# A two-layer graph kernel: waits between stores and between TensorE and VectorE dropped, scatters and loads moved on their queues, and the quantile products placed 22 sorting steps later

## The chip, the cores and the metric

The kernel runs on one core of a Trainium2 chip. A core has five engines with a queue each: TensorE (PE, with its weight loads shown apart as PEld), VectorE (DVE), ScalarE (ACT), GpSimd (POOL) and SyncE (SP), and DMA queues that SP, ACT and POOL start. The metric is the device time of one execution in microseconds (us); what is quoted is the median of several runs. The profile is of one execution of its own.

## The reference, cut to what matters

There are N = 4096 nodes with D = 128 features and a symmetric 0/1 adjacency matrix in which about 1.6% of the entries are set (some 64 neighbours for a node). The first layer is graph attention with 8 heads:

```
Wh  = einsum('nd,hde->hne', nodes, W)
f1, f2 = Wh·a1, Wh·a2
e   = leaky_relu(f1[:, :, None] + f2[:, None, :], 0.2)
att = softmax(where(adj > 0, e, -9e15), axis=-1)
h   = elu(att @ Wh)                       # 8 heads, concatenated: cat
x1  = layernorm(nodes + elu(cat @ W1 + b1))
```

The second layer takes, for each node and feature, three quantiles over the kept neighbours (every m-th neighbour of a list is left out; n_keep remain):

```
svals = sort(where(keep[:, :, None], x1[None, :, :], big), axis=1)
agg   = sum over q in (0.25, 0.5, 0.75) of svals[max(ceil(q * n_keep) - 1, 0)] / 3
agg   = 0.5 * agg + 0.5 * x1
out   = agg @ W.T + b + x1
```

All is in float32 or with integer indices.

## The kernel before, in words

**Stage one, `gat`** (up to about 3,160 us). The nodes are cut into 32 tiles of 128 and into six blocks of 4, 4, 6, 6, 6 and 6 tiles. Two jobs run interleaved.

One is the search for the neighbour lists (class `Front`). SP loads the adjacency in 128 pieces (`a_i`, L378), ScalarE turns them into 0/1 (`nz`, L380), TensorE packs bits into words (L389), and VectorE draws the column numbers out of the words with its instructions for the eight largest (L188, L190). When a block's lists are complete, `place` scatters them to a table `rows_d` in memory (POOL, L541), and further on `keep` makes the lists for the second layer, `meta_d`. This work is cut into some 90 pieces, which `advance(n)` takes from a list `todo`, n at a time; each piece writes its instructions at that place in the program. When all is found, `order` sorts the nodes by the length of their lists, and `late`, 32 calls of `scatter` (L680), writes the sorted order to `order_d`, one POOL DMA for each tile.

The other is attention. It goes over 64 half tiles u. `load(u + 3)` gathers the rows of neighbours three half tiles ahead (POOL, `nb`, L971: 2190 indirect DMAs in all, about 34 for a half tile); at the first tile of a block it also loads the block's list of ids from `rows_d` over SP (L903, and `info`, L932), and `own_row` gathers the nodes' own rows (`me`, L947). `probabilities` makes the softmax (VectorE L1054 to L1103, ScalarE L1073), `rows_sum` multiplies with the rows on TensorE (`ps_z`, L1111), and after two tiles `combine`, a generator of several stages, makes the head outputs, the layer norm, and as its last stage stores the new rows to `x1_d` by two indirect DMAs of POOL (L1197; "x_d" in the profile). After each half tile stands `advance(2)`. `late` is issued when the loads have run out, from u = 61 on, but without an order of its own: the scheduler places it on POOL's queue where its data is ready, and so it stands among the gathers of about 1,920 to 2,027 us.

At the end of `gat` the stages still open are driven to their end. Then a flag is read and a branch taken: to `general` if the lists don't fit the tables (not with this data), else to `sparse`.

**Stage two, `sparse`.** The order is loaded from `order_d` by four DMAs of SP. For each of the 32 tiles in that order, `load(t)` gathers the tile's table row (`info`, POOL L1867), its own rows (`xs`), and HIGH[t] rows of neighbours (`rows`, POOL L1713: 2078 of them), into one of three rotating buffers. A sorting network then runs over the rows' buffer: a step compares k blocks of 128 columns with k others. `compare` copies the lower side into a bank of PSUM on ScalarE (L1751; `low`, two buffers of 16 x 128 columns, or `low_s` in SBUF where k is at most 4), and VectorE writes the minimum (L1756) and the maximum (L1757) back. Steps of which only one side is needed take one instruction and no copy (L1759, L1761). `plan(t)` cuts the network into a first and a second phase, with steps of at most 16 pairs (8 for tile 0); `interleave` orders the second phase of tile t-1 with the first of tile t by modelled times.

After a tile's second phase `quantile` finds the candidates for the three quantiles and weights that are 1 or 0. `pick` returns three parts: `scale` (ScalarE multiplies the candidates by their weights, L1810), `sums` (TensorE adds them up and adds half of x1, L1815 and L1818), and a copy to `comT` (L1823). After four tiles `finish` adds `layer` (three products for each tile, L1835 to L1837) and `layer_copy` (copy to `o`, L1841, and four scatters to `out` on POOL, L1845). These parts wait in a first-in-first-out list, `waiting`. Each two-sided step takes at most one part from its head, right after ScalarE's copy: a part marked "copy" always, a part marked "bank" only where 4 < k <= 12, since it needs the last four of the bank's sixteen column blocks. What is left at the end is issued after the last step.

Of the kernel before, what the change touches and what calls it, by code (L numbers as in the profile page):

```python
# [38 lines left out]
F32 = mybir.dt.float32  # L39
F16 = mybir.dt.float16  # L40
BF = mybir.dt.bfloat16
I32 = mybir.dt.int32
# [3 lines left out]
ALU = mybir.AluOpType  # L46
# [4 lines left out]
P = 128  # L51
N = 4096
# [37 lines left out]
SMALL = 4  # L90
FOUR = 4
CUT = 32
MOST = 16

ENDS = [(t - t % FOUR, FOUR) for t in range(NT - FOUR)]
ENDS += [(NT - FOUR, FOUR - 1)] * (FOUR - 1) + [(NT - 1, 1)]
# [697 lines left out]
    return out  # L794


def gat(tc, nc, c, x, adj, xf_d, meta_d, order_d, flag_d, w, a1, a2, w1, b1, gamma, beta, x1_d):

# [22 lines left out]
    with ExitStack() as ctx:  # L823
# [307 lines left out]
        def combine(t, zT):  # L1131
# [62 lines left out]
            nc.vector.tensor_add(s, s, bc["beta"].unsqueeze(1).to_broadcast(shape))  # L1194
            yield
            for j in range(TWO):
                nc.gpsimd.indirect_dma_start(  # L1197
                    out=x1_d,
                    out_offset=bass.IndirectOffsetOnAxis(ap=index[t + j][3][:, 0:1], axis=0),
                    in_=s[:, j, :],  # L1200
                    in_offset=None,
                )

        held = {u: load(u) for u in range(3)}
        advance(EARLY)
        f1s = {0: spread_f1(0)}
# [3 lines left out]
        for u in range(2 * NT):  # L1210
            t, half = divmod(u, 2)
            if u + 3 < 2 * NT:
                held[u + 3] = load(u + 3)
            elif late:

                advance(len(todo))
                for piece in late:
                    piece()
                late = []
            if not half and t + 1 < NT:  # L1220
                f1s[t + 1] = spread_f1(t + 1)
            ps_z, behind = rows_sum(u, held.pop(u), e)
            if u + 1 < 2 * NT:
                with ExitStack() as order:
                    for ins in behind:
                        order.enter_context(tc.issue_after(ins))
                    e, behind = probabilities(u + 1, held[u + 1], f1s[(u + 1) // 2])
            with ExitStack() as order:
                for ins in behind:
                    order.enter_context(tc.issue_after(ins))  # L1230
                if u % (2 * TWO) == 0:
                    zT = tp.tile([P, H, TWO * P], F32, name="zT")
                collect(u, ps_z, zT)
                for stages in going:
                    next(stages, None)
            if u % (2 * TWO) == 2 * TWO - 1:
                going = going[-1:] + [combine(t - 1, zT)]
            advance(2)
        for stages in going:
            for _ in stages:  # L1240
                pass
        advance(len(todo))


def statistics(tc, nc, c, f_sb, f2m, rows_d):
# [412 lines left out]
def plan(t):  # L1658

    wide = HIGH[t]  # L1660
    extra = wide - MAIN if MAIN < wide <= 80 else 0
    w = wide - extra
    needed = {i - 1 for lo, hi in places(t) for i in range(lo - extra, hi + 1)}
    layers = needed_swaps(swap_layers(w), needed)
    merge = (w - 1).bit_length()

    first = steps(layers[:-merge], lambda i: i, PAIRS if t else PAIRS // 2)
    second = steps(layers[-merge:], lambda i: i)
    if extra:
        apart = needed_swaps(swap_layers(extra), range(extra))  # L1670
        first += steps(apart, lambda i: MAIN + extra - 1 - i)
    return first, second, extra


def sparse(tc, nc, c, x1_d, meta_d, order_d, w, b, out):


    with tc.tile_pool(name="sp1", bufs=1) as one, tc.tile_pool(
# [12 lines left out]
        sixth = one.tile([P, P], F32, name="sixth_i")  # L1691
        nc.scalar.mul(sixth, c["idf"], 0.5 * float(np.float32(1.0 / NQ)))
        wT = one.tile([P, D], F32, name="lwT")
        it = one.tile([P, 2 * MIDDLE], I32, name="it_p")
        nc.gpsimd.iota(it, pattern=[[1, 2 * MIDDLE]], base=0, channel_multiplier=0)
        iota_p = one.tile([P, 2 * MIDDLE], F32, name="iota_p")
        nc.vector.tensor_copy(iota_p, it)
        order = one.tile([P, NT], I32, name="order")
        for i in range(4):
            nc.sync.dma_start(  # L1700
                out=order[:, ts(i, NT // 4)],
                in_=order_d[ts(i, N // 4), :].rearrange("(t p) c -> p (t c)", p=P),
            )

        def bank():
            return psum.tile([P, PAIRS * D], F32, name="low")

# [2 lines left out]
        nc.scalar.copy(wT, ps[:, :D])  # L1710

        def gather(row, info, col):
            nc.gpsimd.indirect_dma_start(  # L1713
                out=row,
                out_offset=None,
                in_=x1_d,
                in_offset=bass.IndirectOffsetOnAxis(ap=info[:, col : col + 1], axis=0),
            )
# [19 lines left out]
        def compare(rows, step):  # L1738


            shape, d, low, high, _ = step
            lows, highs = block(rows, shape), block(rows, shape, d)
            if low and high:
                _, n2, _, n, _, run = shape
                k = n2 * n * run
                if k > SMALL:
                    t = bank()
                else:
                    t = tp.tile([P, SMALL * D], F32, name="low_s", bufs=4)
                packed = block(t, (0, n2, n * run, n, run, run))  # L1750
                nc.scalar.copy(packed, lows)  # L1751
                if waiting and waiting[0][0] == "copy":
                    waiting.pop(0)[1]()
                elif waiting and SMALL < k <= PAIRS - FOUR:
                    waiting.pop(0)[1](t[:, (PAIRS - FOUR) * D :])
                nc.vector.tensor_tensor(lows, packed, highs, op=ALU.min)  # L1756
                nc.vector.tensor_tensor(highs, packed, highs, op=ALU.max)  # L1757
            elif low:
                nc.vector.tensor_tensor(lows, lows, highs, op=ALU.min)  # L1759
            else:  # L1760
                nc.vector.tensor_tensor(highs, lows, highs, op=ALU.max)  # L1761
# [41 lines left out]
        def pick(found, x1, comT):  # L1803

            made = {}

            def scale():
                made["v"] = tp.tile([P, MOST, D], F32, name="picked", bufs=1)
                for i, (v, weight) in enumerate(found):
                    nc.scalar.mul(made["v"][:, i, :], v, weight)  # L1810

            def sums(ps):
                made["ps"] = ps[:, :P]
                for i in range(len(found)):
                    nc.tensor.matmul(  # L1815
                        made["ps"], made["v"][:, i, :], sixth, start=i == 0, stop=False
                    )
                nc.tensor.matmul(made["ps"], x1, half, start=False, stop=True)  # L1818

            return [  # L1820
                ("copy", scale),
                ("bank", sums),
                ("copy", lambda: nc.scalar.copy(comT, made["ps"])),  # L1823
            ]

        def finish(xs, comT, infos):

            m = len(infos)
            made = {}

            def layer(ps):
                made["ps"] = ps
                for j in range(m):
                    to = ps[:, ts(j, D)]
                    nc.tensor.matmul(to, c["idf"], xs[:, j, :], start=True, stop=False)  # L1835
                    nc.tensor.matmul(to, c["ones"][0:1, :], b_row[:, j, :], start=False, stop=False)
                    nc.tensor.matmul(to, comT[:, j, :], wT, start=False, stop=True)  # L1837

            def layer_copy():
                o = tp.tile([P, FOUR, D], F32, name="o")  # L1840
                nc.scalar.copy(  # L1841
                    o[:, :m, :].rearrange("p t d -> p (t d)"), made["ps"][:, : m * D]
                )
                for j, info in enumerate(infos):
                    nc.gpsimd.indirect_dma_start(  # L1845
                        out=out,
                        out_offset=bass.IndirectOffsetOnAxis(ap=info[:, NODE : NODE + 1], axis=0),
                        in_=o[:, j, :],
                        in_offset=None,
                    )  # L1850

            return [("bank", layer), ("copy", layer_copy)]
# [3 lines left out]
        def load(t):  # L1856
            rows = three.tile([P, max(HIGH), D], F32, name="rows")
            first, _ = ENDS[t]
            if t == first:
# [2 lines left out]
                    tp.tile([P, FOUR, P], F32, name="comT"),  # L1862
                    [],
                )
            info = three.tile([P, MW], I32, name="info", bufs=3 * FOUR)
            group[first][2].append(info)
            nc.gpsimd.indirect_dma_start(  # L1867
                out=info,
                out_offset=None,
                in_=meta_d,  # L1870
                in_offset=bass.IndirectOffsetOnAxis(ap=order[:, t : t + 1], axis=0),
            )
            gather(group[first][0][:, t - first, :], info, NODE)
            for s in range(HIGH[t]):
                gather(rows[:, s, :], info, s)
# [377 lines left out]
def gnn(tc, x, adj, w, a1, a2, w1, b1, gamma, beta, lw, lb, out):  # L2253
    nc = tc.nc
    with ExitStack() as ctx:
# [6 lines left out]

        keep = ctx.enter_context(tc.tile_pool(name="keep", bufs=1))
        c = constants(nc, keep)
        gat(tc, nc, c, x, adj, xf_d, meta_d, order_d, flag_d, w, a1, a2, w1, b1, gamma, beta, x1_d)
        other = nc.values_load(flag_d[0:1, 0:1], min_val=0, max_val=1)
        with tc.If(other > 0) as cmp:
            general(tc, nc, c, x, adj, w, a1, a2, w1, b1, gamma, beta, lw, lb, x1_d, out)
        with cmp.Else():
            sparse(tc, nc, c, x1_d, meta_d, order_d, lw, lb, out)  # L2270


_INS = [
# [33 lines left out]
```

## Time and profile before

| | before |
|---|---|
| median of 3 runs | 8432.01 us (8431.48 to 8434.64) |
| the profiled execution | 7646.96 us, of which the span is 7645.2 us |
| instructions | 31290 |
| busy: VectorE | 5831.7 us (76%) |
| busy: GpSimd | 4343.5 us (57%) |
| busy: ScalarE | 2214.1 us (29%) |
| busy: TensorE | 1122.8 us (15%) |
| granted TensorE clock, mean | 0.551 |

The profiled execution is 785 us shorter than the median of the runs. In the lines of the profile, L12 is line 12 of the kernel. A busy row has one digit for each fortieth of the span, 191 us: the busy share in tenths. A line of a group gives the engine, what it writes and reads, how often, then the busy time and the mean in ns of one, then the idle time ahead of the group's instructions, and what ended most of it. A line of the waits gives who waited for whom, the total in us, how many waits, and the longest. A line of the timeline gives start and length in us, and in brackets the idle time before with its releaser; "issue" means that the engine waited for nothing that the profile shows. A DMA that POOL starts shows as POOL's time for issuing it; its landing is later.

### The profile page before, as it was taken

The numbers are of one execution on the slowest core, as the hardware profiler recorded it, in microseconds if no ns is written. First come the engines' busy times: TensorE is split into PE (matmuls) and PEld (weight loads), VectorE is DVE, ScalarE is ACT, GpSimd is POOL, SyncE is SP. The second block draws the span as 40 slices with busy tenths as digits, with TensorE's granted clock in tenths as the row PEclk, the third lists the DMA queues.
The fourth block names the chain that finished last, engine by engine and source line by source line (L and its number), as shares of the span: only waits on it lengthen the run. The fifth ranks groups of instructions, "written<-read, shape, count | busy, mean of one in ns | idle before, by whom it ended". The sixth has DMA issues, their size and how long they took to land. (4 is left out here: it accounts for less than half of the span.)

```text
span 7645.2 us, 31290 instructions
## 1 busy us (share of the span) xinstructions
PE 1122.8 (15%) x6047; PEld 946.8 (12%) x6047; DVE 5831.7 (76%) x9380; ACT 2214.1 (29%) x2301; POOL 4343.5 (57%) x4524
## 2 busy tenths in 40 slices
PE   3243333322222322100000000000000000000001
PEld 1232222222222222100000000000000000000000
DVE  8465555565223222399999999999999999999999
ACT  6020212100000000144344343434334433443433
POOL 2777677777777777565554645455536434554500
PEclk5566666666566666655555555555555555555555
DMA  6242324222222222111111111111101101111100
GB/s 205 57 121 56 107 62 121 60 55 56 47 56 56 56 56 56 40 44 34 40 35 30 41 31 37 30 36 34 38 23 41 34 24 33 36 35 29 33 1 1
DMA packets 219057, 380.95 MB, mean 50 GB/s; under 512 B 129283, under 2 KB 129412, under 8 KB 218852
## 3 DMA queue, kind: packets, MB, share of 16 engines
q0 software_dynamic: 145808, 308.58, 15.3%
q1 hardware_dynamic: 72898, 70.23, 3.1%
q14 instruction: 156, 1.28, 0.1%
q8 instruction: 49, 0.80, 0.0%
q10 hardware_dynamic: 146, 0.07, 0.0%
HBM read 368.26 MB, written 10.31 MB: 50 GB/s over the span
## 5 line engine op out<-in xcount | busy, mean ns | idle before, releaser
L1713 POOL DMA_INDIRECT rows<-x_d,info x2078 | 2018.2, 971 | 1949.5 <-ACT picked L1810 1270.8
L971 POOL DMA_INDIRECT nb<-xf_d,ids x2190 | 2086.0, 953 | 707.0 <-issue 632.2
L1751 ACT COPY low<-rows 128x2048 f32<-128x2048 f32 (+8 forms) x1022 | 1561.5, 1533 | 2429.9 <-DVE rows L1757 1780.7
L1756 DVE TENSOR_TENSOR rows<-low,rows 128x2048 f32<-128x2048 f32 (+9 forms) x1022 | 1884.7, 1862 | 138.9 <-ACT low L1751 50.0
L1757 DVE TENSOR_TENSOR rows<-low,rows 128x2048 f32<-128x2048 f32 (+9 forms) x1022 | 1882.4, 1861 | 5.8
L1054 DVE TENSOR_TENSOR e<-nb,ps_small 128x64 f32<-128x64 f32 (+9 forms) x200 | 47.7, 240 | 1252.6 <-DMA nb<-xf_d,ids 1206.7
L1111 PE MATMUL ps_z<-spread,nb 128*128 128x128 f32 x4500 | 615.7, 305 | 797.9 <-DVE spread L1103 775.6
L1111 PEld LDWEIGHTS ps_z<-spread,nb 128*128 128x128 f32 x4500 | 604.5, 220 | 829.9 <-DVE spread L1103 420.7
L1815 PE MATMUL low<-sixth_i,picked 128*128 128x128 f32 x300 | 79.8, 442 | 4224.7 <-ACT low L1751 3736.4
L1815 PEld LDWEIGHTS low<-sixth_i,picked 128*128 128x128 f32 x300 | 66.8, 324 | 4237.7 <-ACT low L1751 3744.8
L1073 ACT ACTIVATE ps_e<-e 128x256 f32<-128x256 f32 (+4 forms) x64 | 26.1, 408 | 1936.2 <-DVE e L1054 972.6
L1103 DVE TENSOR_TENSOR spread<-e,ps_small 128x1152 f32<-128x1152 f32 (+4 forms) x312 | 342.7, 1107 | 129.2 <-PE ps_z L1111 79.4
L1845 POOL DMA_INDIRECT out<-o,info x32 | 34.4, 1076 | 392.9 <-ACT o L1841 369.2
L380 ACT ACTIVATE nz<-a_i 128x1024 bf16<-128x1024 int32 x128 | 134.3, 1051 | 292.5 <-DMA a_i<-in_adj 254.3
L1751 ACT COPY low_s<-rows 128x512 f32<-128x512 f32 (+3 forms) x325 | 139.8, 471 | 130.5 <-DVE rows L1756 48.0
L389 PE MATMUL ps_words<-nz,pows 128*128 128x512 bf16 (+1 forms) x272 | 113.7, 577 | 364.4 <-ACT nz L387 258.0
L188 DVE MAX8 k<-key 128x8 f32<-128x256 f32 x416 | 164.6, 412 | 0.7
L1756 DVE TENSOR_TENSOR rows<-low_s,rows 128x512 f32<-128x512 f32 (+3 forms) x325 | 158.3, 500 | 3.0 <-ACT low_s L1751 2.1
L1757 DVE TENSOR_TENSOR rows<-low_s,rows 128x512 f32<-128x512 f32 (+3 forms) x325 | 158.7, 500 | 0.3
L190 DVE MATCH_REPLACE8 key<-k,key 128x256 f32<-128x256 f32 x384 | 155.5, 407 | 0.0
L1142 PE MATMUL ps_h<-zT,w_ga 128*128 128x256 f32 x256 | 116.3, 619 | 198.4 <-DVE s L1414 106.6
L1759 DVE TENSOR_TENSOR rows<-rows 128x256 f32<-128x256 f32 (+8 forms) x245 | 141.6, 580 | 0.2
(246 smaller groups left out, 2528.0 us busy)
## 6 DMA issues: line engine op xcount, KB each, us to landing
a_i<-in_adj SPq DMA_DIRECT2D x128, 512.0 KB
nb<-xf_d,ids POOLq DMA_INDIRECT x2190, 2.5
rows<-x_d,info POOLq DMA_INDIRECT x2078, 2.5
xf_d<-xf POOLq DMA_DIRECT2D x4, 576.0 KB, 7.4
xf<-in_x POOLq DMA_DIRECT2D x4, 512.0 KB
meta_d<-rowdata_k SPq DMA_DIRECT2D x4, 324.0 KB
abc_ta<-in_L_gnn_a POOLq DMA_DIRECT2D x2, 512.0 KB, 7.7
w_ga<-in_L_gnn_W POOLq DMA_DIRECT2D x2, 512.0 KB
```

The lines of the kernel that those rows point to most:

```text
L188: nc.vector.max(out=top, in_=work)
L190: nc.vector.match_replace(out=work, in_to_replace=top, in_values=work, imm_value=gone)
L380: nc.scalar.activation(nz[:, j, :], a_i, AF.Relu, scale=-1.0, accum_out=self.negative[:, k : k + 1],)
L971: gather = nc.gpsimd.indirect_dma_start(out=rows[:, used + i, :], out_offset=None, in_=xf_d, in_offset=bass.IndirectOffsetOnAxis(ap=ids[:, ...
L1103: last = nc.vector.tensor_tensor(spread[:, :m], e[:, at : at + m, :].unsqueeze(2).to_broadcast(shape), own.unsqueeze(1).unsqueeze(3).to_br ...
L1111: product = nc.tensor.matmul(ps_z[:, g, :], rows[:, k, :D], spread[:, i].rearrange("p j h -> p (j h)"), start=i0 + i == 0, stop=i0 + i == ...
L1713: nc.gpsimd.indirect_dma_start(out=row, out_offset=None, in_=x1_d, in_offset=bass.IndirectOffsetOnAxis(ap=info[:, col : col + 1], axis=0),)
L1751: nc.scalar.copy(packed, lows)
L1756: nc.vector.tensor_tensor(lows, packed, highs, op=ALU.min)
L1757: nc.vector.tensor_tensor(highs, packed, highs, op=ALU.max)
L1759: nc.vector.tensor_tensor(lows, lows, highs, op=ALU.min)
L1815: nc.tensor.matmul(made["ps"], made["v"][:, i, :], sixth, start=i == 0, stop=False)
```

## The change

1. The stores of x1 are declared independent of each other (`stored`, `declare_no_dep`).
2. The 32 scatters of `order_d` are forced behind the last gather of `nb` in the issue order.
3. `advance(2)` becomes `advance(3)` for u < 16.
4. The constants `it_p` and `iota_p`, the `order` and the `info` of tiles 0 and 1 go to a pool that lives from the start. The loads of the order and the two gathers of `info` stand ahead of the last stages of the last `combine`, thus ahead of the branch; in `sparse`, `load` issues no `info` for these two tiles.
5. In `compare`, the minimum and the maximum of a step are declared independent of the products that TensorE makes in other columns of its bank. `sums` and `layer` return their products for that.
6. Between `scale` and `sums`, 22 parts that do nothing are put into `waiting` (APART); each two-sided step takes one.
7. `plan(0)` cuts the first phase of tile 0 into steps of at most 4 pairs instead of 8.
8. MOST, the room for scaled candidates, is 14 instead of 16; at most 14 are found.

```
-MOST = 16
+MOST = 14
+
+APART = 22
...
-                nc.gpsimd.indirect_dma_start(
+                done = nc.gpsimd.indirect_dma_start(
                     out=x1_d,
...
+                for other in stored:
+                    tc.declare_no_dep(done.ins, other, reason="each node has a row of its own")
+                stored.append(done.ins)
...
                 advance(len(todo))
-                for piece in late:
-                    piece()
+                with tc.issue_after(gathers[2 * NT - 1][HALF - 1, 0]):
+                    for piece in late:
+                        piece()
...
-            advance(2)
-        for stages in going:
+            advance(3 if u < 2 * START[2] else 2)
+        for stages in going[:-1]:
             for _ in stages:
                 pass
-        advance(len(todo))
+
+        for i in range(4):
+            nc.sync.dma_start(
+                out=order[:, ts(i, NT // 4)],
+                in_=order_d[ts(i, N // 4), :].rearrange("(t p) c -> p (t c)", p=P),
+            )
+        for t, info in enumerate(infos):
+            nc.gpsimd.indirect_dma_start(
+                out=info,
+                out_offset=None,
+                in_=meta_d,
+                in_offset=bass.IndirectOffsetOnAxis(ap=order[:, t : t + 1], axis=0),
+            )
+        for stages in going[-1:]:
+            for _ in stages:
+                pass
...
-    first = steps(layers[:-merge], lambda i: i, PAIRS if t else PAIRS // 2)
+    first = steps(layers[:-merge], lambda i: i, PAIRS if t else PAIRS // 4)
...
                 nc.scalar.copy(packed, lows)
+                aside = []
                 if waiting and waiting[0][0] == "copy":
                     waiting.pop(0)[1]()
                 elif waiting and SMALL < k <= PAIRS - FOUR:
-                    waiting.pop(0)[1](t[:, (PAIRS - FOUR) * D :])
-                nc.vector.tensor_tensor(lows, packed, highs, op=ALU.min)
-                nc.vector.tensor_tensor(highs, packed, highs, op=ALU.max)
+                    aside = waiting.pop(0)[1](t[:, (PAIRS - FOUR) * D :])
+                for to, op in ((lows, ALU.min), (highs, ALU.max)):
+                    done = nc.vector.tensor_tensor(to, packed, highs, op=op)
+                    for product in aside:
+                        tc.declare_no_dep(done.ins, product, reason="other columns of the bank")
...
             return [
                 ("copy", scale),
+                *[("copy", lambda: None)] * APART,
                 ("bank", sums),
                 ("copy", lambda: nc.scalar.copy(comT, made["ps"])),
             ]
```

## The prediction

> **What bounds the kernel now.** I read the busy slices first, then the costliest groups, the table of stretches, the waits, and the timeline of single places.
>
> ```profile
> DVE  8465555565223222399999999999999999999999
> POOL 2777677777777777565554645455536434554500
> ...
> L1713 POOL DMA_INDIRECT rows<-x_d,info x2078 | 2018.2, 971 | 1949.5 <-ACT picked L1810 1270.8
> L971 POOL DMA_INDIRECT nb<-xf_d,ids x2190 | 2086.0, 953 | 707.0 <-issue 632.2
> ```
>
> There are two stages. Up to slice 17 (about 3,200 us) VectorE (DVE) is half busy; GpSimd (POOL) is 70 to 80% busy in issuing the gathers of neighbours (L971), and nearly all the rest of its time is its own issue gap. From slice 18 on VectorE is over 90% busy with sorting and POOL's gathers (L1713) wait for free buffers. The stretches give the rate of the first stage:
>
> ```profile
> 400.00:600.00 200.00, 89.43 (x500) 73.08 (x500) 138.19 (x580) 55.07 (x86) 148.07 (x157) 0.66 0.43 119
> ...
> 800.00:1000.00 200.00, 72.75 (x387) 57.51 (x388) 131.91 (x576) 51.95 (x82) 125.85 (x130) 0.62 0.34 98
> ...
> 2200.00:2400.00 200.00, 61.51 (x379) 56.66 (x380) 61.46 (x147) 13.66 (x26) 151.23 (x161) 0.62 0.22 56
> ```
>
> After the stretch stand PE, its loads, DVE, ACT, POOL. A full stretch holds 160 gathers of 0.94 us with 0.30 us between: 1.25 us each, and nothing else fits. Every other POOL instruction among them lengthens the stage by itself; 800 to 1,000 us lost 30 gathers to stalls.
>
> ```profile
> POOL nb L971 <- PE ps_z L1111: 36.9, 8, 21.6
> POOL x_d L1197 <- DMA x_d<-s,info: 14.7, 8, 3.2
> POOL me L947 <- DMA info<-rows_d: 12.3, 3, 4.2
> DVE rows L1756 <- PE low L1837: 20.3, 8, 3.3
> DVE rows L1756 <- PE low L1818: 12.3, 10, 2.2
> SPq L903 <- DMA rows_d<-rowdata,pos_i: 299.0, 5, 95.0
> ```
>
> Total us, number, longest. The first three are POOL's real stalls in stage one, the next two VectorE's waits on TensorE in sorting, the last SP's wait for a block's lists. Then the join of the stages, on POOL:
>
> ```profile
> 3105.62 0.94 POOL L971 DMA_INDIRECT nb<-xf_d,ids  x1 [0.30 <-issue]
> 3146.65 0.98 POOL L1197 DMA_INDIRECT x_d<-s,info  x1 [40.09 <-DVE s L1194]
> 3149.16 0.97 POOL L1197 DMA_INDIRECT x_d<-s,info  x1 [1.52 <-DMA x_d<-s,info]
> 3154.85 0.96 POOL L1197 DMA_INDIRECT x_d<-s,info  x1 [4.72 <-DVE s L1194]
> 3158.36 0.96 POOL L1197 DMA_INDIRECT x_d<-s,info  x1 [2.55 <-DMA x_d<-s,info]
> 3162.02 0.23 POOL L1695 IOTA it_p<- 128x128 int32 x1 [2.71 <-issue]
> ...
> 3170.57 0.94 POOL L1713 DMA_INDIRECT rows<-x_d,info  x1 [0.30 <-issue]
> ```
>
> The last neighbour row leaves at 3105.62; POOL idles 40.09 us for the last rows' result, stores four times, passes the branch, builds indices, and gathers its first row to sort 64.95 us after it.
>
> [...] at 3149.16 POOL stands 1.52 us behind a store with nothing passing it. [...] The kernel has such waits between its stores, though each writes rows of its own; they are the 14.7 us above. [...]
>
> **Part by part**, against the profiled execution's own 7646.96 us (span 7645.2). That is 785 us below the runs' median 8432.01; nothing in the profile says why.
>
> *Order scatters.* Now 32 scatters of order_d stand among the gathers:
>
> ```profile
> L680 POOL DMA_INDIRECT order_d<-node,pos_g x32 | 30.8, 962 | 9.8 <-issue 8.8 <-DMA order_d<-node,pos_g 0.6 <-DVE e L1063 0.3
> ```
>
> (30.8 + 9.8) = 40.6 us of a full POOL. Moved behind the last gather they fill the 40.09 us of idleness: −40.6. Without that cover they would cost all of it again.
>
> *Stores of x1.* The waits between stores go: 14.7 listed and two of 1.5 that the waits book to VectorE, less 1.52 and 2.55 at the join, which are counted below: −13.6.
>
> *The join.* From the last gather: scatters start at 1.25, the last at 1.25 + 31 x 1.27 = 40.6; a scatter landed a median 3.6 us after issue (2.2 to 5.8): 44.2. SP's four loads of the order (0.4 to issue, 2.4 to land): 47. Two info gathers, 47.2 to 49.7. The four stores queue behind them on POOL; their second pair's data is ready at 49.2 in the trace, so they go at 1.25 us: last at 53.5, landed 3.2 later, branch 0.5 (as now), one gather of own rows: first row at 58.4 instead of 64.95: −6.5. What is late next is VectorE's last normalisation, if scatters are quicker.
>
> *A third piece per half tile for u < 16.* In stage one VectorE does 12.5 us of attention per half tile (50 us per 200 us, 43.3 us of POOL per half tile) and pieces of the neighbour lists, 72 in about 608 us: 8.4 each. With three: 12.5 + 25.3 = 37.8 of 43.3 us, 87%. It fits on average, and lists are written earlier: the scatter of block 2's lists stands behind gather 333 instead of 480, of block 1's behind 158 instead of 194. That meets the stalls' root: On SP, L903 waits for the scatter (it now stands behind 87 adjacency loads instead of 79), holds back the loads of the adjacency behind it, and ScalarE with them:
>
> ```profile
> 793.18 1.06 ACT L380 ACTIVATE nz<-a_i 128x1024 bf16<-128x1024 int32 x1 [71.77 <-DMA a_i<-in_adj]
> 799.18 0.46 DVE L1074 TENSOR_TENSOR ps_e<-e,ps_e 128x288 f32<-128x288 f32 x1 [39.36 <-ACT ps_e L1073]
> ```
>
> VectorE then loses 39 us and POOL stalls 8.49 and 21.61 at 820 and 883. Stalls on ps_z over 0.6 us sum to 35.7, on info 12.3: 48 in all. Bounds: −48 (all gone) to +134 (all 16 pulled-forward pieces, 8.4 each, delay POOL). I take −15: a third, since the fuller VectorE makes new ones.
>
> *Waits of sorting on TensorE.* The instruction order shows 39 steps waiting for TensorE before, none after: −(20.3 + 12.3) = −32.6. The wait can move to ScalarE: the copy of a result (comT, o) comes right behind the next step's copy, and the layer's 24 products take 7.9 us (4224.45 to 4232.3). ScalarE has slack (slices of 40%) and sums come 24 to 28 steps, about 80 to 110 us, after the scaling, so their data is never late; I put back 7.6 for eight layers: −25. Bounds −32.6 and 0. Empty pops cost nothing: they emit no instruction.
>
> *Tile 0 in steps of 4 pairs.* 83 steps with 99.1 us of VectorE for 46 with 88.6 (counted from the plan, with the trace's times): +10.5 of work, but VectorE idles 20.10, 10.07 and 13.95 us for rows there, and smaller steps start on fewer rows. −5, bounds −10 and +10.5.
>
> *Tail.* 22 steps behind, the last loop's 14 both-sided steps run out: the sums of tile 30, its copy, the last full layer and its output fall behind the last comparison at 7632.88. Nine products at 0.67 (6 us), and output scatters that go 2.8 us apart, partly beside the last tile's: +5, bounds +2 and +10.
>
> Preload and pool moves else cost nothing: the index constants (0.23 us on POOL) now start the kernel beside loads.
>
> Sum: −40.6 −13.6 −6.5 −15 −25 −5 +5 = −100.7, to 7546 in the profile's execution. On the runs, −101 if a stall is as long there, −111 if the 10% is spread evenly: 8432 − 106 = about 8326; I say 8325.
>
> **Rivals.**
> *A, everything goes:* stalls 48, waits 32.6, tile 0 −10, tail +2, the rest the same: −149, about 8280. For it: block 2's lists are 147 gathers (184 us) earlier. Against: VectorE at 87%.
> *B, the waits come back:* TensorE's wait becomes ScalarE's (0), stalls stay (0), tile 0 +10.5, tail +10, the rest −60.7: −40, about 8390. [...] Against: its slack.
> *C, VectorE becomes the bound early:* 87% busy leaves 5.5 us per half tile, 88 us over 16. If ScalarE's stalls (39 to 48 us each, three in the trace) remain, or pieces cost over 10.3 us each beside (12.5 + 3 x 10.3 = 43.3), POOL waits for spread matrices, and the pulled-forward pieces show in full: +134 − 101 = +33, about 8465. Against: the pieces gone from later halves leave nothing to overfill, and POOL runs three half tiles ahead.
> *D, the change doesn't do what it says:* scatters still among gathers, or the waits kept. The built order speaks against it; at most some effects cancel, 8432.
>
> **How the numbers follow.** Forecast (−60 to −135) 0.62, 8325; A (to −185) 0.13, 8280; B (−20 to −60) 0.13, 8390; C 0.07, 8465; D 0.05. About 0.2% (17 us) is what a measurement tells from no change. Range 8250 to 8412 holds the forecast, B and most of A; C, D and A's end are out, 0.15. Faster 0.88, same 0.05, slower 0.07.
>
> **What would show it.** Full stretches of 160 gathers around 1,950 us and 32 scatters behind the last gather; no POOL wait for a store; first sorting gather about 58 us after the last neighbour row; no VectorE wait on TensorE; last tile's products, one full layer and its outputs behind the last comparison. It is wrong if POOL's waits on ps_z grow in 200 to 900 us, if VectorE's waits on ScalarE grow by as much as those on TensorE fall, or if the tail passes 20 us.

## The result, and the profile after

The changed kernel took 8382.62 us (8371.12 to 8386.41), the kernel before 8433.33 (8431.48 to 8440.11): ratio 0.9939, interval 0.9924 to 0.9954. That is 51 us faster, where 107 were forecast. The profiled execution took 8386.41 us, span 8384.6. It agrees with the runs, which the profile before did not. One thing must be known to read any number below: executions come in two kinds, one in which the kernel before takes 8377 to 8433 us and one in which it takes 7644 to 7648, and the profile before is of the second kind, the result of the first. The page of the changed kernel, first kind:

```profile
DVE  6454564454222222224899999999999999999899
...
POOL 3545546656666666666455456445554545354410
...
L1726 POOL DMA_INDIRECT rows<-x_d,info x2078 | 2031.9, 978 | 1863.7 <-ACT picked L1826 1184.2
L975 POOL DMA_INDIRECT nb<-xf_d,ids x2190 | 2078.1, 949 | 1329.5 <-issue 625.3
```

Stage one now reaches slice 18 of longer slices: the last neighbour gather leaves at 3739 us instead of 3106. A gather costs POOL what it did (949 ns, 953 before), and its own issue gap is the same (625 us, 632 before); to that come 704 us of other idleness, where there were 75. The stretches and the waits say where they are:

```profile
400.00:600.00 200.00, 53.68 (x316) 43.38 (x315) 114.47 (x499) 46.72 (x74) 95.53 (x101) 0.62 0.30 87
800.00:1000.00 200.00, 48.89 (x206) 37.33 (x206) 97.77 (x424) 34.47 (x53) 112.59 (x119) 0.59 0.26 74
2200.00:2400.00 200.00, 66.21 (x306) 58.09 (x307) 49.33 (x124) 11.17 (x21) 129.56 (x138) 0.59 0.19 48
```

```profile
POOL nb L975 <- PE ps_z L1115: 508.2, 33, 58.5
POOL nb L975 <- remote: 170.6, 36, 9.4
```

No stretch is full any more (101, 119, 138 instructions of POOL where 160 fit): POOL waits 679 us for buffers that TensorE has yet to read. ("Remote" is a release whose origin the profile doesn't show; 35 of these 36 waits are on a semaphore that in this trace TensorE alone raises.) TensorE's own lines at one place of stage one, where the profile shows nothing that it waits for:

```profile
2185.80 1.95 PE L1115 MATMUL ps_z<-spread,nb 128*128 128x128 f32 x16
2188.36 0.27 PE L1115 MATMUL ps_z<-spread,nb 128*128 128x128 f32 x1 [0.61 <-issue]
2191.16 0.27 PE L1115 MATMUL ps_z<-spread,nb 128*128 128x128 f32 x1 [2.53 <-issue]
2193.96 0.37 PE L1115 MATMUL ps_z<-spread,nb 128*128 128x128 f32 x1 [2.53 <-issue]
2196.75 0.37 PE L1115 MATMUL ps_z<-spread,nb 128*128 128x128 f32 x1 [2.42 <-issue]
...
2210.05 0.37 PE L1115 MATMUL ps_z<-spread,nb 128*128 128x128 f32 x1 [0.33 <-issue]
2210.75 0.37 PE L1115 MATMUL ps_z<-spread,nb 128*128 128x128 f32 x1 [0.33 <-issue]
2211.45 1.87 PE L1115 MATMUL ps_z<-spread,nb 128*128 128x128 f32 x8 [0.33 <-issue]
```

After 16 products in 1.95 us one comes every 2.80 us, with a weight load halfway (the first at 2189.75): an instruction every 1.40 us. Later the products come 0.70 us apart, then eight in 1.87 us. I call such a stretch the grid. ScalarE and VectorE fall on it too: at tile 0, shown below, their starts after a wait are 1.40, 4.20 or 5.60 us apart. The profile before has no such gap at any of its products; summed over the trace, the gaps of this kind (0.3 to 2.6 us, at products that wait for nothing) are 592 us here.

### The profile page after: what moved, and what is told of

The parts are those of the page before. It is cut to its first block, busy times and chain, and to the rows that moved or that the text cites. A ratio compares the mean times of both kernels' runs of the same rounds, so it can differ in the third digit from the quotient of the medians.

```text
span 8384.6 us, 31455 instructions
## 1 busy us (share of the span) xinstructions
PE 1235.7 (15%) x6047; PEld 1032.2 (12%) x6047; DVE 5886.7 (70%) x9454; ACT 2218.9 (26%) x2338; POOL 4358.1 (52%) x4524
## 5 line engine op out<-in xcount | busy, mean ns | idle before, releaser
L1771 DVE TENSOR_TENSOR rows<-low,rows 128x2048 f32<-128x2048 f32 (+10 forms) x1970 | 3649.3, 1893 | 88.0 <-ACT low L1764 61.7
L1764 ACT COPY low<-rows 128x2048 f32<-128x2048 f32 (+8 forms) x985 | 1528.4, 1557 | 2331.8 <-DVE rows L1771 1665.3
L1115 PE MATMUL ps_z<-spread,nb 128*128 128x128 f32 x4500 | 757.9, 325 | 1491.4 <-issue 737.3
L1115 PEld LDWEIGHTS ps_z<-spread,nb 128*128 128x128 f32 x4500 | 702.4, 237 | 1565.9 <-issue 996.7
L1771 DVE TENSOR_TENSOR rows<-low_s,rows 128x512 f32<-128x512 f32 (+3 forms) x798 | 395.3, 523 | 128.7 <-remote 39.9
L1764 ACT COPY low_s<-rows 128x512 f32<-128x512 f32 (+3 forms) x399 | 179.8, 486 | 281.6 <-DVE rows L1771 172.0
L1873 POOL DMA_INDIRECT out<-o,info x32 | 34.9, 1091 | 397.2 <-ACT o L1869 369.3
L1130 ACT COPY zT<-ps_z 128x512 f32<-128x512 f32 x64 | 37.6, 587 | 742.7 <-remote 586.0
L190 DVE MAX8 lists<-cand 128x8 f32<-128x176 f32 x416 | 128.1, 332 | 69.7 <-remote 47.1
L1438 DVE SCALAR_TENSOR_TENSOR zT<-zT,ps_h 128x512 f32<-128x512 f32 x64 | 42.0, 682 | 158.0 <-ACT zT L1437 109.7
```

Source lines behind the costliest of these rows:

```text
L190: nc.vector.max(out=top, in_=work)
L1115: product = nc.tensor.matmul(ps_z[:, g, :], rows[:, k, :D], spread[:, i].rearrange("p j h -> p (j h)"), start=i0 + i == 0, stop=i0 + i == ...
L1771: done = nc.vector.tensor_tensor(to, packed, highs, op=op)
```

## The experiments

The runs form five sets, each on a chip of its own beside the kernel before, and all runs of a set met the same kind. Sets one and two (chips 2 and 5) met the first kind, with the grid; three and four (chips 1 and 15) the second, without; five (chip 10) the first again.

**The kernel before, unchanged.**

> The kernel before, unchanged, for a profile in the state of the timed runs. Theory G (grid): the profile of the changed kernel shows stretches in which TensorE, and ScalarE and VectorE too, start one instruction every 1.40 us; the timed runs of the kernel before have them too and its profile of 7647 us lacks them. Then this profile is about 8430 us long, its last neighbour gather leaves at about 3750 to 3800 us instead of 3106, POOL waits some 600 us on ps_z in stage one, and stage two is about as long as in the changed kernel, 4500 to 4550 us. Rival S (stage two): the first stage gained what was forecast and the change itself lengthened sorting by some 80 us. Then the last gather leaves near 3850 us and stage two takes about 4450 us.

8388.47 us beside 8389.51; span 8372.6. The last neighbour gather left at 3643.8, POOL waited 561 us for TensorE (369.3 on ps_z, 191.5 "remote"), TensorE's slow gaps are 631 us. So the grid is there without the change, as theory G said, though the last gather left over 100 us earlier than G put it. Stage two is another matter: from the first comparison to VectorE's last 4635.8 us, not the 4500 to 4550 that G expected. VectorE's waits there:

```profile
DVE rows L1756 <- remote: 178.0, 8, 41.9
DVE rows L1756 <- ACT low L1751: 36.1, 33, 2.3
...
DVE rows L1756 <- PE low L1818: 12.0, 8, 2.5
...
DVE rows L1756 <- PE low L1837: 3.3, 1, 3.3
```

Seven of the first row's eight are of 16 to 42 us, one for each four tiles, where a layer's products stand; the profile before had eight of up to 3.3 us there. One of them:

```profile
4802.88 2.16 DVE L1756 TENSOR_TENSOR rows<-low,rows 128x1920 f32<-128x1920 f32 x1 [1.83 <-ACT low L1751]
4846.93 1.09 DVE L1756 TENSOR_TENSOR rows<-low,rows 128x896 f32<-128x896 f32 x1 [41.89 <-remote]
```

The layer's last products on TensorE start at 4807.11 by the same trace:

```profile
4807.11 0.80 PE L1837 MATMUL low<-lwT,comT 128*128 128x128 f32 x2
```

VectorE gets on 39.8 us later. So there was far more to win in sorting than the 32.6 us of the profile before.

**The edits of stage one alone** (stores, scatters, third piece, preload; MOST 14 with them, for room in SBUF).

> The kernel before with the edits of stage one alone (stores independent, scatters behind the last gather, three pieces per half tile, the order and two table gathers ahead of the branch). G: stage one is held by TensorE's slow issue, so what is taken from POOL between gathers is covered: 10 to 40 us faster. S: the whole 61 to 76 us forecast for these edits, 8355 to 8372.

8470.6 us, ratio 1.010 (1.0083 to 1.0117): 81 us slower than before. Both theories fail.

**The edits of stage two alone** (no waits on products, APART, tile 0 in steps of 4; MOST 14).

> The kernel before with the edits of stage two alone (no waits on products, 22 empty parts, tile 0 in steps of 4 pairs). G: the waits on TensorE, which the slow issue lengthens, go: 10 to 40 us faster. S: 10 to 30 us slower than before.

8264.58 us, ratio 0.9852 (0.9835 to 0.9868): 125 us faster, three times G's upper end. The two halves sum to −44, the change as a whole gave −51: the halves add up, and the first takes back most of what the second gives.

**Two pieces instead of three.**

```
-            advance(3 if u < 2 * START[2] else 2)
+            advance(2)
```

> The changed kernel with two pieces per half tile for u below 16 instead of three. G: VectorE is not what holds stage one, so within 15 us of the changed kernel (8370 to 8400). Rival V (VectorE too full with three): 8320 to 8360. If earlier lists are worth something: 8395 to 8430.

8256.69 us, ratio 0.9847 (0.983 to 0.9863): 133 us faster than before, so the third piece costs about 80. That is rival V's direction, by more than its range. The waits until the 700th neighbour gather, first of the changed kernel (142 to 1444 us), then with two pieces (142 to 1303 us):

```profile
POOL nb L975 <- PE ps_z L1115: 316.5, 15, 58.5
...
PE ps_z L1115 <- DVE spread L1107: 254.8, 15, 57.4
```

```profile
POOL nb L975 <- PE ps_z L1115: 208.1, 13, 37.2
...
PE ps_z L1115 <- DVE spread L1107: 177.8, 18, 41.6
```

POOL waits for TensorE, TensorE for VectorE's spread matrices, and VectorE is in a piece. Against the kernel before, the gathers with three pieces (edits of stage one alone) were 98 us late at the 500th, 142 at the 900th, and 78 at the 1300th, when the pieces had run out: only a part is given back. With two pieces they were 2, 6 and −8 us off.

**Tile 0 in steps of 8 pairs again, with two pieces.**

> The changed kernel with two pieces per half tile and tile 0 in steps of 8 pairs as before. In the traces so far the small steps of tile 0 cost about 62 us of VectorE's idleness in the first 200 us of sorting (109 against 47) and start it 7.5 us earlier. Theory T (the small steps cost more than they bring): about 50 us faster than with steps of 4 pairs, 8190 to 8220. Rival: the slow stretch only moves on to the next tile, and the time stays within 15 us of 8257.

8176.15 us, ratio 0.9758 (0.9742 to 0.9775), some 70 us better still, more than theory T's 50; its rival falls. In the changed kernel tile 0 looks like this:

```profile
3991.44 0.43 DVE L1771 TENSOR_TENSOR rows<-low_s,rows 128x256 f32<-128x256 f32 x1 [2.70 <-remote]
3992.84 1.63 DVE L1771 TENSOR_TENSOR rows<-low_s,rows 128x512 f32<-128x512 f32 x3 [0.97 <-DVE rows L1771]
3997.04 2.38 DVE L1771 TENSOR_TENSOR rows<-low_s,rows 128x512 f32<-128x512 f32 x4 [2.57 <-remote]
4002.64 0.69 DVE L1771 TENSOR_TENSOR rows<-low_s,rows 128x512 f32<-128x512 f32 x1 [3.23 <-remote]
4004.04 1.90 DVE L1771 TENSOR_TENSOR rows<-low_s,rows 128x512 f32<-128x512 f32 x3 [0.71 <-issue]
4008.24 0.69 DVE L1771 TENSOR_TENSOR rows<-low_s,rows 128x512 f32<-128x512 f32 x1 [2.30 <-issue]
```

The starts after a wait are multiples of 1.40 us apart (1.40, 4.20, 5.60, 1.40, 4.20). ScalarE's copies from 3999.20 us on start 1.40 or 4.20 us apart as well: the two hand over small steps on the grid. In the first 200 us of sorting VectorE idles 109 us; with steps of 8 pairs 48.

**The place without the freedom, and the freedom without the place.** First the edits of stage two with

```
-APART = 22
+APART = 0
```

> The edits of stage two alone, with APART 0: the products lie right behind the scaling again, but VectorE still doesn't wait for them. Theory N (dropping the wait is what pays): within 20 us of the edits of stage two alone, 8245 to 8285. Theory P (the place pays: ScalarE[...] takes over the wait as it copies comT right behind the products): 40 to 110 us slower, 8305 to 8375.

8393.54 us, ratio 1.0019 (1.0012 to 1.0026). Then APART at 22, with the two lines that declare minimum and maximum independent of the products left out:

> The edits of stage two alone, with the 22 empty parts but with VectorE's waits on the products kept. Theory N: the layer's products still hold VectorE some 20 us eight times, so most of the gain is gone, 8360 to 8420. Theory P: the products are ready early and nothing is held, 8255 to 8300.

8313.9 us, ratio 0.9927 (0.9911 to 0.9944). With both the ratio was 0.9852. Each result lies outside the ranges of both theories. N falls; P has the better of it but isn't the whole. Without the place the waits come back under another name. The table of waits without it:

```profile
DVE rows L1760 <- ACT low L1753: 116.9, 31, 30.0
DVE rows L1760 <- issue: 110.8, 35, 41.9
```

VectorE's seven long waits stand where they stood, now of 13 to 42 us. The profile puts four to ScalarE and three to nobody ("issue"); in all seven ScalarE stands idle for 16 to 44 us at the copy of a layer's result to `o`, so this is rival B's mechanism. With the place alone two long waits are left (16.3 and 21.3 us), with both as well (13.7 and 22.5, behind ScalarE). All three kernels carry tile 0's small steps. If these cost the same 70 us in each, an estimate from the run above, the waits are worth about 200 us with both, 135 with the place alone, 55 with the freedom alone.

**The scatters back among the gathers, with two pieces.**

> The changed kernel with two pieces per half tile and the 32 order scatters placed by the scheduler among the gathers again. The trace says that moving them took 41 us off the gathers, and that at the same time the join of the stages grew by 33 us. If both belong to the scatters' place: stage one +41 and join -33, so 8245 to 8275. If the join grew for another edit (the two table gathers ahead of the last stores, the order of the last stages): 8285 to 8310.

8260.35 us, ratio 0.9858 beside 0.9847 (intervals ±0.0017): no difference that can be told. The trace shows both halves of the expectation: the last gather leaves 43 us later, and the join is 55.1 us instead of 89.6. First the join with the scatters behind the last gather, then with them among the gathers:

```profile
3609.09 0.94 POOL L975 DMA_INDIRECT nb<-xf_d,ids  x1 [0.30 <-issue]
3683.92 0.99 POOL L1201 DMA_INDIRECT x_d<-s,info  x1 [25.01 <-DVE s L1198]
3698.71 0.96 POOL L1726 DMA_INDIRECT rows<-x_d,info  x1 [1.53 <-ACT lwT L1723]
```

```profile
3651.87 0.94 POOL L975 DMA_INDIRECT nb<-xf_d,ids  x1 [0.30 <-issue]
3693.31 0.99 POOL L1201 DMA_INDIRECT x_d<-s,info  x1 [40.50 <-DVE s L1198]
3706.96 0.96 POOL L1725 DMA_INDIRECT rows<-x_d,info  x1 [0.31 <-ACT lb L1711]
```

**Scatters spread thin, and the layer's copy put off.** These four, set three, met the second kind (before 7648.23 us), though most of their expectations were for the first.

> Two pieces per half tile, tile 0 in steps of 8 pairs, and the 32 order scatters two behind the gathers of each half tile from u = 43 on, instead of all behind the last gather. POOL waits some 6 us per half tile for a buffer. Theory W (any instruction fits into that wait): the gathers leave as early as with the scatters behind them, the join is 55 us as where the scatters were free, so 30 to 40 us faster than 8176. Rival R (TensorE only catches up while POOL rests, so the wait is not free time): the 41 us of the scatters come back, within 15 us of 8176.

7577.96 us, ratio 0.9909; repeated beside the others of that kind below.

> Two pieces per half tile, tile 0 in steps of 8 pairs, and eight more empty parts between the layer's products and the copy of their result. In the trace of that kernel two waits of VectorE on ScalarE's copies, 13.7 and 22.5 us, stand behind a layer. If the copy of the result o, which comes one step behind the products, is what ScalarE stands for: both go, 25 to 40 us faster than 8176, 8135 to 8152. If not: within 10 us of 8176.

7613.95 us, ratio 0.9955 (0.9939 to 0.9972), where the same without the eight parts has 0.9866. The waits it aimed at don't exist without the grid, and the list now falls behind: the tenth tile's scaling starts at 4401 us instead of 4352. As I read it, the rows' buffers then come free late; ScalarE's waits for gathered rows rise from 58 to 149 us, and VectorE idles 27 and 24 us in two places. A list that is emptied in order must fit the loop.

> Two pieces, tile 0 in steps of 8, order scatters placed freely among the gathers, and 32 further scatters of the same values to a table of its own, which nothing reads, behind the last gather. Read from the trace, from the last neighbour gather to the first gather of rows to sort: 55 us with nothing there, 89 us with the order scatters there. Theory Q (while POOL issues DMAs back to back, the other engines stay on the grid of 1.40 us): 85 to 92 us. Rival: the growth came from the loads that wait for the order, and with scatters that nobody waits for it is 55 to 62 us.

> The same with 76 short index fills (some 40 us of POOL without a DMA) behind the last gather in place of the further scatters. If any work of POOL keeps the other engines on the grid: 85 to 92 us from the last neighbour gather to the first gather of rows. If only its DMAs do: 55 to 62 us.

The join was 55.2 and 55.3 us, in one execution of each: without the grid neither 40 us of DMAs nor the fills make it longer than the 55.1 us above. The fills took 23 us, not the 40 that were meant.

**The change and its parts without the grid** (before 7643.81 us).

> The changed kernel, unchanged. Without the grid of 1.40 us (before at 7648): the sum of the prediction, 7546, corrected by what the runs without the grid showed (stage two 27 us better than forecast, nothing from the stores and the stalls): 7540 to 7580. With the grid (before at 8377 to 8433): ratio 0.993 to 0.995.

> The changed kernel with two pieces per half tile. Without the grid: VectorE has room for the third piece (37.8 of 43.3 us), so within 15 us of the changed kernel. With the grid: 75 to 90 us faster than it.

> Two pieces, and tile 0 in steps of 8 pairs. Without the grid: small steps are worth their start, so 0 to 10 us slower than with steps of 4. With the grid: 65 to 85 us faster.

> The same with two order scatters behind each half tile's gathers from u = 43 on. Without the grid: 30 to 45 us slower than with all behind the last gather, since POOL is full there. With the grid: POOL waits for TensorE anyway and the join is shorter; theory W 30 to 40 us faster, rival R (TensorE catches up only while POOL rests) within 15 us.

Changed kernel 7523.99 us, ratio 0.9843 (0.9827 to 0.986): 120 us faster, and better than expected. Two pieces 7536.01: the third gains 12. Steps of 8 in tile 0 7541.74: small steps gain 6. (The four runs of each lie apart, but the intervals of the three ratios overlap, so these two gains are small and uncertain.) Scatters spread 7578.91: 37 slower than all behind the last gather. The page and the join of the changed kernel, to be held against those of before:

```profile
DVE  8587776532232232499999999999999999999998
...
POOL 2767777777777777775454554555536435554500
```

```profile
3041.77 0.94 POOL L975 DMA_INDIRECT nb<-xf_d,ids  x1 [0.30 <-issue]
3043.02 0.99 POOL L682 DMA_INDIRECT order_d<-node,pos_g  x1 [0.30 <-issue]
...
3090.29 1.00 POOL L1258 DMA_INDIRECT info<-meta_d,order  x1 [7.05 <-DMA order<-order_d]
3091.59 0.96 POOL L1258 DMA_INDIRECT info<-meta_d,order  x1 [0.30 <-issue]
3092.85 0.99 POOL L1201 DMA_INDIRECT x_d<-s,info  x1 [0.30 <-issue]
...
3100.45 0.96 POOL L1726 DMA_INDIRECT rows<-x_d,info  x1 [0.30 <-issue]
```

POOL never waits for a store, and the first row to sort is gathered 58.7 us after the last neighbour row.

**POOL's stream in the join, with the grid** (before 8419.42 us).

> Two pieces, tile 0 in steps of 8, order scatters placed freely among the gathers, and 32 further scatters to a table that nothing reads behind the last gather. From the last neighbour gather to the first gather of rows, with the grid (before at 8377 to 8433): theory Q, POOL's stream of DMAs keeps the other engines on the grid: 85 to 92 us; rival, the growth came from the loads that wait for the order: 55 to 62 us. Without the grid (before at 7645): 55 us, as in the run before.

From 3690.92 to 3775.69, in one execution: 84.8 us. The rival falls; Q's range is missed by 0.2 us. Nobody waits for these scatters, yet the last normalisation comes 30 us after their end:

```profile
3690.92 0.94 POOL L976 DMA_INDIRECT nb<-xf_d,ids  x1 [0.30 <-issue]
...
3731.35 0.96 POOL L1230 DMA_INDIRECT again_d<-node,pos_g  x1 [0.30 <-issue]
3761.85 0.96 POOL L1202 DMA_INDIRECT x_d<-s,info  x1 [29.54 <-DVE s L1199]
...
3775.69 0.96 POOL L1739 DMA_INDIRECT rows<-x_d,info  x1 [0.30 <-ACT lb L1725]
```

> Two pieces, tile 0 in steps of 8, two order scatters behind each half tile's gathers from u = 43 on. With the grid, against the ratio 0.976 with all scatters behind the last gather: theory W (POOL's waits are free time) 0.971 to 0.973; rival R (TensorE catches up only while POOL rests) 0.974 to 0.978. Without the grid: 0.991 as before.

8234.49 us, ratio 0.9782 (0.9765 to 0.9798), against 0.9758 with all behind the last gather, in another set. W falls: POOL's waits for buffers aren't free time. The join, with no scatter in it, was 55.7 us.

## Why the prediction was wrong, by its steps

In us against before; without the grid from the traces (spans 7645.2 and 7521.4) and medians, with it from the medians of the parts and some traces, which carry some ±15.

| step | forecast | without the grid | with the grid |
|---|---|---|---|
| order scatters off the gathers | −41 | −50 | −43, and +34 in the join |
| waits between stores | −14 | +2 | about 0 |
| third piece, stalls | −15 | −16 (median −12) | about +80 |
| the join else | −6.5 | −6.3 | −10 |
| sorting's waits on TensorE | −25 | −54 | about −200 |
| tile 0 in steps of 4 | −5 | −6 | about +70 |
| tail | +5 | +6.6 | +7 |
| sum | −101 | −124 | about −60 (measured −51) |

**The failing step** is the one that names the scale: "785 us below the runs' median 8432.01; nothing in the profile says why", and then adding the saving of that execution to the runs, at most stretched by 10%. The 785 us weren't spread evenly. By the two profiles of the kernel before, 538 us lay ahead of the last neighbour gather and 190 in sorting. They lay in the grid: TensorE's products in stage one and waits behind the layer in stage two. In an execution of the profile's kind the sum was near (−124), but not by all its terms: the stores brought nothing, and sorting's waits brought twice their term.

With the grid three terms were far off: the third piece by about +95, tile 0 by +75, sorting by −175. That the measured 8383 lies within the stated 8250 to 8412 is luck, since these errors mostly cancel.

**Third piece.** The prediction put −15, since three pieces of 8.4 us and 12.5 of attention fill 37.8 of 43.3 us, and rival C named the point: pieces over 10.3 us. Summed over the trace of the kernel before with the grid, 200 to 1300 us, the pieces' instructions are 420 us busy and VectorE idles 258 us ahead of them: (420 + 258) x 8.4 / 420 = 13.6 us for a piece, an estimate of mine. That is past the point as it was put, but the point itself moves: POOL's half tile is 57.4 us in that window instead of 43.3, of which three such pieces and 12.5 of attention are 53.3, before the idleness of attention is counted. What shows VectorE as the holder is the run with two pieces and the waits on `spread` above. One group of the pieces' instructions in the page of the profile before, and in that of the kernel before with the grid:

```profile
L188 DVE MAX8 k<-key 128x8 f32<-128x256 f32 x416 | 164.6, 412 | 0.7
```

```profile
L188 DVE MAX8 k<-key 128x8 f32<-128x256 f32 x416 | 168.5, 415 | 153.3 <-remote 106.9
```

Busy the same, idle ahead of it 0.7 and 153.3 us. C's mechanism held in this part, with +80 in place of its full +134; C's time (8465) did not come, since sorting gave more. (C's sum also kept the −15 of the third piece beside the +134; without it C stood at 8480.) The prediction's own sign of being wrong came true with the grid: POOL's waits on ps_z from 200 to 900 us grew from 117 (before) to 203 us; without the grid they fell from 35 to 26. That lists come earlier was right and worth little: SP's waits at the load of a block's lists for their scatter fell from 96 us (before, with the grid) to 28.

**Sorting's waits.** Mechanism right, size off twice. Without the grid no wait of VectorE on TensorE is left in sorting, the 7.6 us put back didn't come, and its waits on ScalarE fell as well (50.0 to 32.3 us). With it the waits were 178 + 12.0 + 3.3 us instead of 32.6. That a step and the products, in columns of their own, need no wait for each other was my assumption; what the runs show is the time that dropping the wait brings, 0.9852 beside 0.9927 with it kept, both with APART at 22.

**Stores.** They freed nothing. With the grid, at the 1200th gather, ahead of the scatters, one run with two pieces stands 6 us late and another 11 early. Without it the two kernels with two pieces whose order scatters stand among the gathers, as before, send the last gather at 3108.04 and 3107.86 us; the kernel before sent it at 3105.62. POOL's waits on ps_z took back 8 us with two pieces (36.9 to 44.8); where the rest went is open.

**Scatters.** The saving held: −43 with the grid, −50 without (the last gather at 3057.66 where a kernel that is the same up to there, but with the scatters among the gathers, has 3108.04). The cover held only without the grid. With it POOL's idleness at the join was not free: with 32 scatters in it POOL still stood 25.0 us for the last normalisation (40.5 without them), and the first row to sort came 34 us later.

**Tile 0 and tail.** Tile 0's sign held only without the grid; +10.5 was the bound I gave, for work alone, and hand-overs on the grid cost 70. The tail was right.

**What stays open.** What makes the grid, and why one set met it and another not, no run shows. Each set had one chip and one time, so the chip or whatever else went on at that time may decide it; no chip on record met both kinds. The mean granted clock gives no answer: in the kernel before it was 0.60 with the grid and 0.62 without from 200 to 3000 us, and 0.50 in both from 4000 to 7500 us, where the long waits stood in one alone.

What is shown is that at the join the grid comes with POOL's stream of DMAs: the join is 84.8 to 89.6 us with 32 DMAs in it and 55.1 without, and 55.2 with them where there is no grid. Where POOL rested, the grid cost nothing: the join of the kernel before is 64.85 us with it and 64.95 without. Elsewhere the link is weaker. In four of the seven longest waits of sorting before (over 15 us), VectorE got on 7 to 9 us after POOL paused; but POOL itself waited there for a buffer (`xs`) that the layer's products read, and both got on within 2 us of each other. In the other three POOL made no pause of over 1.5 us near, so POOL's stream is not all of it. Whether short fills without a DMA do the same wasn't tried with the grid.

Of the versions run, two pieces with tile 0 in steps of 8 has the best ratio with the grid (0.9758) and 0.9866 without, where the changed kernel has 0.9843: it beats the kernel before in both, and the changed one where the grid is.

## What to carry to other kernels

When the profiled execution and the median of the runs differ by more than the change could bring, find what the difference is made of before pricing anything: here a profile of the slower kind would have turned two of the signs. Price work that is put in front of a late consumer by its wall time, idle gaps included, and look for the point from which it decides. Give products distance to the instruction that reads them as well as freedom for the instructions that don't: here, with the grid and by the estimate above, freedom alone brought some 55 us, distance alone 135, both 200.

## What the runs showed of the hardware

- There are stretches, 23 us in the lines above, in which TensorE starts an instruction every 1.40 us, later a product every 0.70 us, with nothing to wait for that the profile shows; VectorE's small steps start on the same grid (1.40, 4.20 and 5.60 us apart). Such gaps are 592 us of TensorE's time in the changed kernel's trace and 631 in the trace of the kernel before with the grid; the profile before has none. Busy times differ by less than 1% between the profile before and that of the changed kernel: VectorE 5831.7 and 5886.7 us, ScalarE 2214.1 and 2218.9, GpSimd 4343.5 and 4358.1.
- VectorE's wait behind a layer's 24 products took up to 41.9 us with the grid, 39.8 of them after the last products had started by the trace; without the grid it took up to 3.3.
- A gather costs POOL the same in both (949 ns with the grid, 953 without, 0.30 us between two).
